# Two of the seven products of the first FFN matmul get a second level of Strassen's scheme, from the second group of tokens on

## The chip, the cores and the metric

The kernel runs on one core of one Trainium2 chip. The metric is the device time of one execution in microseconds (us); lower is better. Before the change the median of three runs is 941.86 us (941.83 to 941.86). Everything is float32.

## The reference

The program is a state-space convolution along the sequence, a routed low-rank FFN, and a residual:

```python
u = conv(x * mask, k) * mask              # x: 64 x 64 x 1024, one kernel per head
xf = u.reshape(4096, 1024)
scores = xf @ Wr.T                        # 64 experts
top_vals, top_idx = top_k(scores, 16)
G = zeros(4096, 64).at[rows, top_idx].set(softmax(top_vals))
h = einsum('nd,krd->nkr', xf, A)          # first FFN matmul: 4096 x 1024 by 1024 x 1024
out = einsum('nkr,kdr->nd', h * G[:, :, None], B) * 2   # second FFN matmul
return x + out
```

## The kernel before, in words

The 4096 tokens are worked in eight groups `g` of 512 (eight heads by 64 batches). For each group the kernel makes the convolution (`conv`), the gates (`gates`, `spread_gates`) and the first FFN matmul (`first`, which runs `seven`). When all groups are through, a second stage (`second`) does the second FFN matmul; the change does not alter its work.

**The first FFN matmul** of a group multiplies the 1024 x 1024 matrix A with the group's 1024 x 512 activations `y`. It uses one level of Strassen's scheme in Winograd's form: A and `y` are cut into 2 x 2 blocks, and seven products of a 512 x 512 left factor with a 512 x 256 right factor take the place of eight. The left factors are the list `wa`; they are made once, partly by DMAs that accumulate, issued from GpSimd (`third_sum`, `fourth_sum`, L230 to L239). The right factors `rf` are four blocks of `y` and their sums `t1`, `t2`, `t4` and `b12`, made on VectorE for each group (`right_factors`).

`seven` is called twice per group, for `j` = 0 and 2: each call does 256 of the 512 rows of every product. In one call a product is eight `nc.tensor.matmul`s (two row blocks of 128 by four blocks of the contraction), each with a 128 x 128 stationary block and 256 moving columns, into one PSUM bank of the four of pool `ps_f`. In the profile each such matmul stands as two MATMUL records and two LDWEIGHTS records, so one product of one `j` is 16 MATMULs (L687). The order in a call is product 1 (bank `c11`), 6, 2 (added to `c11`), 7, 5 (bank `c12`), 4, 3 (added to `c12`). VectorE takes the banks up as they end: `u2 = p1 - p6` (L709), `u3 = p7 + u2` (L716), `c22 = -u3 - c12` (L503), then in `finish` `u3 = p4 - u3` (L492) and `u2 = c12 + u2` (L1052).

`finish` multiplies the four blocks by the gates: one on VectorE (`first_quarter`, L1041), three on GpSimd (L1034). It puts them, and four sums of them (`sums`, VectorE, L492), into the tile `hg`, of which there is one buffer, and stores `hg` to HBM by DMAs from GpSimd's queue (`store`, L1037). The first write to the next `hg` waits until those stores have landed.

**The order of the work.** A scheduling layer fixes each engine's instructions in one static order at build time; each engine runs its own in that order and waits on semaphores. The generators `first` and `conv` are stepped alternately, so that TensorE goes through convolution matmuls of group g+1 between products of group g. Around the change TensorE's order in the middle groups is: the transposes of the gate scores (`psc`, L959), the rest of the products for `j` = 2, the first products of the next group, the convolution's matmuls (`pc`, L828, L836, L851) for head pairs 0 and 1, more products, `pc` for pairs 2 and 3, the state matmuls (`pu`, L742) of the following group, the score matmuls (`psh`, L947), again `pu`, and `psc`.

VectorE's order holds, in the same span: the choice of 16 experts out of `psc` (L961 to L984), the recursion of the states (L786), `right_factors`, the uptake of the products, the tables of the next kernels (`rf`, `rk`, `rsn`, `bt`, and for three of the groups `f`, `k`, `w`), and the uptake of the convolution `y = pc * mask` (L862), which frees the banks that `pu` is written to.

GpSimd's queue holds, in order: the DMAs that make the left factors, then for each group the eight loads of spread gates (`gx`, L1007), the gate multiplications and the stores. In group 0 the order of `first_quarter` is pinned (`late_gates`).

Of the kernel before, what the change touches and what calls it, by code (L numbers as in the profile page):

```python
# [107 lines left out]
def body(ctx: ExitStack, tc, x, xo, lens, par, dvec, dgrp, at, bm, wt, cst, out):  # L108
# [18 lines left out]
    fp = pool(ctx, "fp", 2, "left")  # L127
    gp = pool(left, "gp", 1, "left")
    tq = pool(left, "tq", 1, "left")
    ids = pool(ctx, "ids", 1, "right")  # L130
    const = pool(right, "const", 1, "right")
    xp = pool(right, "xp", 4, "right")
# [369 lines left out]
    def stt(o, a, s, o1, b, o2):  # L502
        V.scalar_tensor_tensor(out=o, in0=a, scalar=s, in1=b, op0=o1, op1=o2)  # L503
        return o
# [169 lines left out]
        tt(t4, b21, t2, ALU.subtract)  # L674
        return b11, b21, b22, t4, t1, t2, b12

    def seven(fac, rf, j, name, finish, second_early=False):

        def product(n, bank=None, more=False):
            first = bank is None
            if first:
                bank = ps_f.tile([P, 2, HT], F32, tag="pf", name=f"{name}_{j}_{n}")
            for ii in range(2):
                for k in range(KH):
                    nc.tensor.matmul(  # L687
                        bank[:, ii, :],
                        lhsT=fac[n - 1][:, k, (j + ii) * P : (j + ii + 1) * P],
                        rhs=rf[n - 1][:, k, :],  # L690
                        start=(first and ii == 0 and k == 0),
                        stop=(ii == 1 and k == KH - 1 and not more),
                        skip_group_check=True,
                    )
            return bank

        def new(t, n=0):
            return fp.tile([P, 2, HT], F32, tag=t, name=f"{name}_{j}_{t}{n}")

        c11 = product(1, more=True)  # L700
        p1 = new("p", 1)
        marks["p1"] = nc.scalar.copy(p1, c11)
        yield
        if second_early:
            product(2, c11)
            yield
        p6 = product(6)
        u2 = new("u2")
        marks["u"] = V.tensor_tensor(out=u2, in0=p1, in1=p6, op=ALU.subtract)  # L709
        yield  # L710
        if not second_early:
            product(2, c11)
            yield
        p7 = product(7)
        u3 = new("u3")
        marks["u"] = V.tensor_tensor(out=u3, in0=p7, in1=u2, op=ALU.add)  # L716
        yield
        c12 = product(5, more=True)
        c22 = new("p", 5)
        stt(c22, u3, -1.0, ALU.mult, c12, ALU.subtract)  # L720
        yield
        p4 = product(4)
        yield
        product(3, c12)
        finish(j, c11, u2, u3, c12, p4, c22)
        yield


    begun = {}
# [284 lines left out]

    hg_dram = dram.tile([NG, P, 7, KH, HT], F32, tag="hg", name="hg_dram")

    def first(g, y, spread):
# [4 lines left out]
        if g:  # L1024
            rf[:] = right_factors(v, f"ty{g}_")

        def finish(j, c11, u2, u3, c12, p4, c22):
            hg = hp.tile([P, 7, 2, HT], F32, tag="hg", name=f"hg_{g}_{j}")

            def gate(m, s):  # L1030
                return spread[m, j][:, :, s * HT : (s + 1) * HT]
# [1 line left out]
            def gt_(o, a, b, op):  # L1033
                G.tensor_tensor(out=o, in0=a, in1=b, op=op)  # L1034

            def store(a, b):
                nc.gpsimd.dma_start(hg_dram[g, :, a:b, j : j + 2, :], hg[:, a:b])  # L1037

            b11, b21, b22, t4, t1, t2, b12 = (hg[:, n] for n in range(7))
            def first_quarter():  # L1040
                i = V.tensor_tensor(out=b11, in0=c11, in1=gate(0, 0), op=ALU.mult)  # L1041
                if late_gates:
# [4 lines left out]
            if not late_gates:  # L1047
                first_quarter()
            gt_(b22, c22, gate(1, 1), ALU.mult)
            tt(u3, p4, u3, ALU.subtract)  # L1050
            gt_(b21, u3, gate(1, 0), ALU.mult)
            marks["u"] = V.tensor_tensor(out=u2, in0=c12, in1=u2, op=ALU.add)  # L1052
            gt_(b12, u2, gate(0, 1), ALU.mult)
            if late_gates:
                first_quarter()
            store(0, 3)

            def sums():
                tt(t1, b11, b12, ALU.subtract)
                tt(b12, b22, b12, ALU.subtract)  # L1060
                tt(t2, b22, t1, ALU.add)
                tt(t4, b21, t2, ALU.subtract)
                store(3, 7)

            unsummed.append(sums)

        for j in range(0, KH, 2):
            for n, _ in enumerate(seven(wa, rf, j, f"h{g}", finish, g + j == 0)):
                if n == 1:
                    sum_factors()  # L1070
                yield
                if n == 1 and len(rf) == 2:

                    rf[:] = right_factors(v, f"ty{g}_")

    unsummed = []

    def sum_factors():
        while unsummed:
            unsummed.pop()()  # L1080


    def second_level(f, e):
# [12 lines left out]

    def load_factor(sg, n, halves):
        for gg in range(2):
            queued(halves[gg], hg_dram[2 * sg + gg, :, n - 1])

    def second_sums(r, u1, u2, u4, pinned=False):

# [249 lines left out]
    for g in range(NG):  # L1352
        ex = gates(g, y)
        if g:
            spread = {}
            for _ in steps:
                pass
            if g + 1 == NG:
                right.close()
                wpb = pool(ctx, "wpb", 1, "right")  # L1360
                wb_quarters = quarters(wpb, bm, "wb", nc.sync)
                ahead(products, 13 - done[0])
                spread_gates(g, ex, spread)
            for _ in products:
                pass
            products, done = counted(first(g, y, spread)), [0]
        if g + 1 == NG:
            break
        ahead(products, (1, 3)[g] if g < 2 else 2)
        spread_gates(g, ex, spread)  # L1370
        if g == 0:
# [140 lines left out]
```

## Time and profile before

| | |
|---|---|
| median of three runs | 941.86 us |
| the profiled execution, its own time | 941.79 us |
| span of its instructions | 940.0 us |
| granted TensorE clock | 1.00 throughout |
| MATMULs of the first FFN matmul (L687) | 1792, 224 for each group |
| first FFN matmul on the chain that ended last | 39% of the span |
| second FFN matmul (L1272) on that chain | 35% |

Times in the profile are in us unless marked ns. PE is TensorE's matmuls, PEld its weight loads, which run beside matmuls; DVE is VectorE, ACT ScalarE, POOL GpSimd, SP the queue of SyncE. A name such as h<-y,was reads: written, then read, with numbers left out; h are the banks of the first FFN matmul, waa and was the left factors, ty and y the right factors, s the states. A group's line gives the count, the busy time, the mean duration in ns of one, and the idle time of the engine before them with what ended it. Durations of back-to-back instructions overlap, so what one costs in a full queue is the step from its start to the next start, not its duration. The chain that ended last is followed back from the last instruction, at each step to what released it.

### The profile page before, as it was taken

How to read it: one execution, taken by the hardware profiler on the slowest of the kernel's cores; microseconds unless marked ns; L12 is line 12 of the kernel's file. 1: busy time of each engine (PE TensorE's matmuls, PEld its weight loads, DVE VectorE, ACT ScalarE, POOL GpSimd, SP SyncE). 2: the span in 40 equal slices, each digit the busy share in tenths (PEclk: the TensorE clock that was granted, in tenths of full speed). 3: DMA queues.
4: the chain of work that ended last, by engine and by line, in shares of the span. 5: the costliest groups of instructions: out<-in, count | busy, mean ns of one | idle time of the engine just before them, and what ended most of it. 6: DMA issues, size and time to landing. Idle time of an engine off the chain costs nothing.

```text
span 940.0 us, 14255 instructions
## 1 busy us (share of the span) xinstructions
PE 929.5 (99%) x5384; PEld 743.2 (79%) x5384; DVE 741.0 (79%) x1725; ACT 164.1 (17%) x314; POOL 337.0 (36%) x284
## 2 busy tenths in 40 slices
PE   7999999999999999999999999999999999999998
PEld 2576768688588588588588788888888888888887
DVE  8899798797996995995892497879856866785674
ACT  5343233411411411510300000000000000000000
POOL 0113213052052052052052032356746555764555
PEclk9999999999999999999999999999999999999999
DMA  8635335347454444444242463754672574358332
GB/s 291 186 87 168 107 110 156 108 126 189 125 144 154 124 138 159 125 128 169 90 131 101 152 246 124 255 203 140 212 275 79 191 270 155 110 205 307 95 123 101
DMA packets 72298, 149.47 MB, mean 159 GB/s; under 512 B 10054, under 2 KB 21030, under 8 KB 72230
## 3 DMA queue, kind: packets, MB, share of 16 engines
q1 hardware_dynamic: 52546, 99.65, 32.1%
q0 software_dynamic: 16864, 47.22, 16.0%
q10 hardware_dynamic: 2820, 1.70, 0.6%
q8 instruction: 42, 0.69, 0.3%
q14 instruction: 26, 0.21, 0.1%
HBM read 100.13 MB, written 47.33 MB: 157 GB/s over the span
## 4 chain that ended last, share of the span: by engine, by line
PE 93%; DVE 6%; issue 0%; DMA 0%; ACT 0%; DVEq 0%
PE h L687 39%; PE s L1272 35%; PE pu L742 5%; PE pc L851 4%; PE psh L947 3%; PE pc L828 3%; PE pc L836 1%; DVE bt L492 1%; DVE hg L492 1%; DVE f L492 1%; DVE f L503 0%; PE psc L959 0%; PE pb L440 0%; PE last L1272 0%; DMA par_sb<-in_par 0%
## 5 line engine op out<-in xcount | busy, mean ns | idle before, releaser
L786 DVE SCALAR_TENSOR_TENSOR s<-s,turn 128x64 f32<-128x64 f32 (+1 forms) x432 | 122.8, 330 | 2.8 <-ACT s L747 2.3
L687 PE MATMUL h<-y,waa 128*128 128x256 f32 x512 | 116.7, 380 | 0.0
L687 PE MATMUL h<-y,was 128*128 128x256 f32 x512 | 116.2, 379 | 0.0
L687 PE MATMUL h<-ty,was 128*128 128x256 f32 x512 | 116.0, 379 | 0.0
L687 PEld LDWEIGHTS h<-y,waa 128*128 128x128 f32 x512 | 96.3, 190 | 15.0 <-issue 1.9
L687 PEld LDWEIGHTS h<-ty,was 128*128 128x128 f32 x512 | 97.1, 190 | 13.9 <-issue 0.8
L687 PEld LDWEIGHTS h<-y,was 128*128 128x128 f32 x512 | 96.8, 190 | 13.7 <-DVE b L503 0.4
L1034 POOL TENSOR_TENSOR hg<-h_p,gx 128x512 f32<-128x512 f32 x16 | 35.6, 2223 | 141.6 <-DVE h_p L503 107.1
L1007 POOL DMA_DIRECT2D gx<-gt_dram x56 | 33.9, 618 | 145.1 <-DMA gt_dram<-gt 145.1
L1286 ACT COPY p<-s 128x512 f32<-128x512 f32 x28 | 16.4, 585 | 312.4 <-PE s L1272 312.4
L1034 POOL TENSOR_TENSOR hg<-h_u,gx 128x512 f32<-128x512 f32 x32 | 45.1, 1409 | 63.8 <-DVE h_u L492 36.6
L1131 POOL TENSOR_TENSOR o<-o,acc_a 128x512 f32<-128x512 f32 x32 | 47.6, 1506 | 41.4 <-ACT acc_a L1149 32.5
L687 PE MATMUL h<-ty,waa 128*128 128x256 f32 x256 | 58.4, 381 | 0.0
L687 PEld LDWEIGHTS h<-ty,waa 128*128 128x128 f32 x256 | 48.2, 190 | 8.3 <-DVE rsn L492 0.8
L742 PE MATMUL pu<-x,bt 128*64 128x448 f32 x256 | 53.0, 546 | 0.4
L862 DVE TENSOR_TENSOR y<-pc,mask 128x512 f32<-128x512 f32 x64 | 40.2, 680 | 16.4 <-PE pc L851 16.4
L1131 POOL TENSOR_TENSOR o<-o,b_room 128x512 f32<-128x512 f32 x32 | 49.1, 1555 | 9.8 <-DVE b_room L492 9.8
L492 DVE TENSOR_TENSOR o<-o,s 128x512 f32<-128x512 f32 x50 | 34.1, 681 | 23.0 <-PE s L1272 17.9
L1037 POOL DMA_DIRECT2D hg_dram<-hg x32 | 25.6, 800 | 67.4 <-DVE hg L492 46.6
L1131 POOL TENSOR_TENSOR o<-o,u 128x512 f32<-128x512 f32 x36 | 45.3, 1282 | 10.0 <-DVE u L492 9.7
L492 DVE TENSOR_TENSOR hg<-hg 128x512 f32<-128x512 f32 x64 | 42.4, 682 | 4.7 <-POOL hg L1034 4.3
L1272 PE MATMUL s<-qy,wbs 128*128 128x256 f32 x192 | 44.1, 379 | 0.0
(275 smaller groups left out, 1678.8 us busy)
## 6 DMA issues: line engine op xcount, KB each, us to landing
x<-in_x SPq DMA_DIRECT2D x32, 512.0 KB
hg_dram<-hg POOLq DMA_DIRECT2D x16, 1024.0 KB, 6.0
o<-in_xo SPq DMA_DIRECT2D x64, 256.0 KB
out<-o SPq DMA_DIRECT2D x63, 256.0 KB
gx<-gt_dram POOLq DMA_DIRECT2D x56, 256.0 KB, 4.8
qy<-hg_dram SPq DMA_DIRECT2D x28, 512.0 KB
r<-hg_dram SPq DMA_DIRECT2D x26, 512.0 KB
hg_dram<-hg POOLq DMA_DIRECT2D x16, 768.0 KB, 4.5
```

What stands on the lines that cost most here:

```text
L492: V.tensor_tensor(out=o, in0=a, in1=b, op=o_)
L687: nc.tensor.matmul(bank[:, ii, :], lhsT=fac[n - 1][:, k, (j + ii) * P : (j + ii + 1) * P], rhs=rf[n - 1][:, k, :], start=(first and ii == ...
L742: nc.tensor.matmul(pu[hh * NS : (hh + 1) * NS, :], lhsT=bt[:, i, (1 - c) * P + hh * NS : (1 - c) * P + (hh + 1) * NS], rhs=xt[:, hh, : NCH ...
L786: return V.scalar_tensor_tensor(out=o, in0=a, scalar=scalar, in1=b, op0=op0, op1=op1)
L828: nc.tensor.matmul(pcs[hh][half_of(e, 1), chunks(e)], lhsT=toep[:, 2 * i + hh, HP:], rhs=xt[:, hh, chunks(e)], start=True, stop=False, ski ...
L851: m = nc.tensor.matmul(pcs[hh][half_of(e, late), into], lhsT=w[o : o + NS, c, i, seg : seg + HP], rhs=s[o : o + NS, c, of].rearrange("p k ...
L862: marks["y"] = V.tensor_tensor(out=y[:, :, i // 2, 2 * (i % 2) + hh, :], in0=pcs[hh].rearrange("p (k b) -> p k b", b=NB), in1=mask, op=ALU ...
L947: nc.tensor.matmul(phalf[o : o + NE, :], lhsT=wt_sb[:, d, :], rhs=yf[:, d, :], start=(d < 2), stop=(d >= NBLK - 2),)
L1007: i = queue.dma_start(gx[:, ii, :], gt_dram[g, c * n : (c + 1) * n, :].unsqueeze(1).to_broadcast([n, RANK, TOK]),)
L1034: G.tensor_tensor(out=o, in0=a, in1=b, op=op)
L1131: tc.keep_in_program_order(G.tensor_tensor(out=o, in0=a, in1=b, op=op_))
L1272: nc.tensor.matmul(bank[:, ii, :], lhsT=left_[i - 1][:, k, ii * P : (ii + 1) * P], rhs=right_[i - 1][:, k, :], start=(first and ii == rows ...
```

## The change

From group 1 on (`LOW_FROM`), products 7 and 4 are no longer done as 512 x 512 by 512 x 256 in two calls. Each is done once per group, as a whole, by a second level of the same scheme (`low`): seven products of a 256 x 256 left factor with a 256 x 128 right factor. Each of the seven is four matmuls, with 128 moving columns in place of 256. The other five products stay as they were.

For this:

- `left_factors` makes the left factors of the second level for `wa[6]` and `wa[3]` once, in group 0, by fourteen DMAs from GpSimd's queue: for each, three copies and an accumulation, two more accumulations, and a last one (in place, after group 0 has used the factor) that is issued at the start of group 1. The first twelve stand on the queue ahead of the `gx` loads of group 0.
- `low_rights` makes the right factors on VectorE: four sums of 128 x 256 for each of the two products in each group.
- `low` does the seven small products and hands their banks to `early` and `late`: seven more VectorE instructions of 128 x 256 for each, and one copy on ScalarE.
- `seven` is one generator over both `j`. Product 7 is done at `j` = 0 and its result kept in two `u3` tiles; product 4 is begun after `j` = 0 and its second half is finished among the products of `j` = 2 (`open_`).
- The gated block `b21` and the sum `t4` come later; they are multiplied and stored apart (`done`, `last_sum`). `hg` has six places in place of seven, each half is stored by four DMAs in place of two, and the order of the factors in HBM follows `SLOT`.
- A pool `lop` holds the new factors, and `dynamic_dma_scratch_size` is 2048 in place of its default.

```diff
+    def left_factors(n):
+        f, h = wa[n - 1], L // 4
+        e = lop.tile([P, 3, 2, h], F32, tag=f"e{n}", name=f"low_{n}")
+        a11, a12, a21, a22 = f[:, :2, :h], f[:, 2:, :h], f[:, :2, h:], f[:, 2:, h:]
+        s1, s2, s4 = e[:, 0], e[:, 1], e[:, 2]
+        for o, a in ((s1, a21), (s2, a11), (s4, a12)):
+            add(o, a)
+        for o, a in ((s1, a22), (s2, s1), (s4, s2), (a21, a11)):
+            add(o, a, accum_op=ALU.add)
+            yield
+    def low_rights(r, name):
+        e = lop.tile([P, 3, 2, H2], F32, tag="r", name=name)
+        tt(u1, r11, r12, ALU.subtract)
+        tt(u2, r22, u1, ALU.add)
+        tt(r12, r22, r12, ALU.subtract)
+        tt(u4, r21, u2, ALU.subtract)
+    def low(n, rights, name, early, late):
+        c11 = product(1, more=True)
+        nc.scalar.copy(v2, c11[:, :, :H2])
+        q6 = product(6)
+        tt(v2, v2, q6[:, :, :H2], ALU.subtract)
+        early(v2)
+        q7 = product(7)
+        tt(v3, q7[:, :, :H2], v2, ALU.add)
+        product(2, c11)
+        late((0, 0), c11[:, :, :H2], None, None)
+        yield
+        c12 = product(5, more=True)
+        late((1, 1), c12[:, :, :H2], v3, v2)
+        q4 = product(4)
+        late((1, 0), q4[:, :, :H2], v3, v3)
+        product(3, c12)
+        late((0, 1), c12[:, :, :H2], None, None)
...
+            steps_ = iter(())
+            if lows and not j:
...
+                steps_ = low(7, low_rights(rf[6], f"{name}_r7"), name, early, late)
+                next(steps_)
+                yield j
...
+            if lows and j:
+                for half, v in zip((lo_, hi_), fourth_of):
+                    tt(u3[:, :, half], v, u3[:, :, half], ALU.subtract)
...
-            store(0, 3)
+            store(0, 2, 0)
...
+            def last_sum():
+                tt(b11, b21, t2, ALU.subtract)
+                store(0, 1, 6)
+            def done(u3):
+                gt_(b21, u3, gate(1, 0), ALU.mult)
+                store(2, 3, 2)
+                unsummed.extend((sums, last_sum))
...
+        if g == 0:
+            made_left = [left_factors(n) for n in (7, 4)]
+            for steps_ in made_left:
+                ahead(steps_, 3)
```

## The prediction

> **What bounds the kernel now.** I read the page first, its busy shares and its chain, and then asked for the waits of TensorE. From the page and from the whole chain in order of time:
>
> ```profile
> PE 929.5 (99%) x5384; PEld 743.2 (79%) x5384; DVE 741.0 (79%) x1725; ACT 164.1 (17%) x314; POOL 337.0 (36%) x284
> DVE  8899798797996995995892497879856866785674
> PE 93%; DVE 6%; issue 0%; DMA 0%; ACT 0%; DVEq 0%
> ...
> 68.60 0.88 PE pb L440 x8
> 253.41 34.53 PE h L687 x160
> ```
>
> TensorE is busy 99% of the span, so a matmul left out shortens the run if nobody else becomes late. The digits of DVE say that somebody could: up to the 24th slice VectorE is near 80 to 90%. A table by stretch makes that plain (span, then busy time of PE, PEld, DVE, ACT, POOL, clock, DMA):
>
> ```profile
> 223.00:294.00 71.00, 70.88 (x470) 54.36 (x470) 61.13 (x168) 18.46 (x33) 18.64 (x18) 1.00 0.46 141
> 436.00:507.00 71.00, 71.00 (x476) 54.52 (x469) 54.91 (x149) 9.09 (x18) 18.99 (x19) 1.00 0.37 120
> ```
>
> One group takes 71 us of TensorE and 55 to 61 us of VectorE. That is not yet slack to spend: both run in a fixed order, and VectorE's free time may lie elsewhere than where TensorE waits for it. The chain across one turn of a middle group shows that VectorE is already on the path there:
>
> ```profile
> 229.93 0.04 DVE h_u L1052
> 230.54 2.35 DVE bt L492 x2
> 242.24 0.61 DVE y L862
> 242.89 3.23 PE pu L742 x16
> 252.72 0.59 PE psc L959 x4
> 253.41 6.69 PE h L687 x31
> ```
>
> From the last product at 229.93 to the end of the first uptake of `y` VectorE works 12.9 us without a break; `pu` needs that bank and starts at 242.89, just as TensorE's own matmuls run out. The same chain stands at 301 and at 372.
>
> **The gain on TensorE.** A whole product is 2 x 16 MATMULs per group; at 34.53 / 160 = 0.2158 us that is 6.91 us. By the second level it is 7 x 4 matmuls, 56 records of 128 columns. No row has such a matmul with an ordinary stationary block. Nearest are the transposes of L440, which also move 128 columns and load a new 128 x 128 block each time:
>
> ```profile
> L687 PE MATMUL h<-y,waa x512: 379/379/483, 39.6 to 583.0; 128*128 128x256 f32 x171
> L440 PE MATMUL pb<-cst_sb,b x32: 270/272/332, 19.8 to 174.7; 128*128 128x128 f32 x32
> L687 PEld LDWEIGHTS h<-y,waa x512: 186/190/192, 39.6 to 582.8; 128*128 128x128 f32 x171
> L440 PEld LDWEIGHTS pb<-cst_sb,b x32: 137/139/143, 19.8 to 174.6; 128*128 128x128 f32 x32
> ```
>
> Eight of them take 0.88 us, 0.110 each. Their weight load takes 139 ns, that of a product 190, so this is the lower bound: 56 x 0.110 = 6.16, a gain of 0.75 us a product. Upper bound, if loads followed each other at their full duration: 56 x 0.190 = 10.64, a loss of 3.73. A load seems to cost less than its duration: the first matmul of a product behind other work takes 483 ns, not 379, so a load that nothing covers costs 104 ns, and that fits under 110. I take 0.110: 14 products (two in each of seven groups) x 0.75 = **10.4 us gained**; range +52 to -10.4.
>
> Here a rule speaks against the change. The Trainium skill, page "TensorE: Matmul & The Clock Gate", section "Back-to-back issue gap", says that in pairs of weight load and matmul both set the spacing, and gives some 81 ns at 128 columns where a lone matmul would take 56. By that ratio 0.110 would be 0.16, a product 8.9 us, and the change would lose 28 us on TensorE alone; the transposes, in pairs too, do not show it.
>
> **What VectorE gets.** From its timeline after `psc`, and the group beside it:
>
> ```profile
> 254.26 0.68 DVE L961 TENSOR_REDUCE sc<-psc 128x256 f32<-128x512 f32 x1
> ...
> 257.95 0.41 DVE L492 TENSOR_TENSOR sb<-sb,sc 128x256 f32<-128x256 f32 x1
> 258.28 0.41 DVE L492 TENSOR_TENSOR sa<-sc,m 128x256 f32<-128x256 f32 x1
> 258.62 0.67 DVE L1041 TENSOR_TENSOR hg<-h,gx 128x512 f32<-128x512 f32 x1
> ...
> 265.67 0.67 DVE L503 SCALAR_TENSOR_TENSOR h_p<-h_u,h 128x512 f32<-128x512 f32 x1
> ```
>
> From start to start a 128 x 256 instruction costs 0.335 us and a 128 x 512 one 0.60 (258.62 to 259.22). Per group the two small schemes bring 22 of the first kind, `j` = 2 brings two more and one `u3 + u2` of 0.60, and four of 0.60 go (L716 and `p4 - u3`, twice): 24 x 0.335 + 0.60 - 2.40 = 6.2 us. 61.1 + 6.2 = 67.3 of a turn of 69.5: by sums it fits, with 3% to spare. So I went along both engines' new order and looked at each place where TensorE waits for VectorE.
>
> *a. The second half of product 4, behind `psc`.* TensorE now comes from `psc` and its small transpose (0.55 us), through small products 5 and 4 (0.88 each) and half of product 6 (1.73), to small product 3 at 4.04 us after `psc`'s start; it needs `late((1, 1))` on VectorE, which the order puts behind the choice of experts. VectorE starts that 1.54 us after `psc` (252.72 to 254.26), needs 3.5 us to 257.75, and 0.335 for the uptake: 5.4. TensorE waits 1.4 us; in the fourth such turn, where `sc` starts 1.08 after `psc`, 0.9. Before, 3 x 3.46 us of products covered the same work.
>
> *b. `c22` before product 3 of `j` = 2.* Before, product 4 (3.46 us) lay between product 5, which feeds `c22`, and product 3, which overwrites its bank. Now 1.30 us of product 1 of the next group do. VectorE reached `c22` 11.4 us after `sc` (254.26 to 265.67). In the new order 1.0 of small uptakes, 0.60 of `last_sum` and 0.60 and more of `u3` and `u2` come ahead: 14.1, and 0.6 to do it, 16.3 after `psc`. TensorE is there at 14.8 + 1.4 = 16.2. But `last_sum` stands in VectorE's queue too, and waits for GpSimd's multiplication of `b21` (1409 ns, L1034), which can start only when the last uptake is done; only 0.86 us of recursion lies between. About 0.8 more, and all behind it on VectorE waits with it: 0.9 us.
>
> *c. `u2` before small product 7.* From `c22` to `u2` VectorE has 11.0 us in the new order (four sums of `right_factors` at 1.14, `sums`, `low_rights` of 1.3), TensorE 10.8, with small product banks to be freed by it: 0.7, with one 1.86 us instruction for 1.14 where GpSimd is multiplying.
>
> *d. The uptake of `y`.* The 12.9 us chain above gets four small uptakes and loses L709: 12.9 + 1.34 - 0.60 = 13.6. On TensorE three small products (2.64) replace product 6 (3.46): 12.1 in place of 12.96. It waits 1.5 us, in the three turns that have the `f` tables.
>
> Sum: three turns at 1.4 + 0.9 + 0.7 + 1.5 = 4.5 are 13.5; one turn without tables 0.9 + 0.9 + 0.7 = 2.5; the first two groups and the last have the same pairs in other places: 2.2 each for the two, 1.6 for the last, by half of the others. Together **24 us lost**; bounds 9 (only *d* and half of *a*) and 38 (each added instruction with two SBUF inputs once beside a multiplication, as bt<-rsn,rf at 231.13 took 1.68 for 0.60, twice a group).
>
> **GpSimd's queue in group 0.** Twelve DMAs come ahead of the `gx` loads:
>
> ```profile
> 49.63 0.88 POOL L239 DMA_DIRECT2D was<-was  x1 [1.03 <-DMA was<-in_at]
> 67.62 4.83 POOL L1007 DMA_DIRECT2D gx<-gt_dram  x8 [17.11 <-DMA gt_dram<-gt]
> ```
>
> Each factor is a chain of copy, accumulation, accumulation, each waiting for the landing before it. At 4.8 us to landing (`gx`, page, 256 KB) two chains take 29 us: from 50.5 to 80 at least, where `gx` now starts at 67.6. At 3.5, the shortest landing of `gx` in that stretch, 72. VectorE stands at `first_quarter` of group 0 (73.69, pinned) until `gx` lands, so 4 to 14 us longer, with the recursion for group 1 behind it. TensorE needs that recursion at 92.72 and has it at 86.98: 5.7 are covered. It costs 0 to 8 us; I take 4, the middle. The two accumulations in place of group 1 cost nothing: 1.5 us of issue in a queue idle for 64% of the span, under two products; uncovered, 10 us once. Two more stores for each half of `hg`, 0.8 us of issue each, lie in the same idle time, except the wait in *b*. ScalarE's two copies (0.35 us, 83% idle) are covered by the small product between. The later `t4` is read in the second stage only.
>
> The smaller DMA scratch (2048) shows in no row. If it lets GpSimd issue a transfer only after the one before has landed, a store holds GpSimd for its 6.0 us landing (page) and not for 0.8 of issue; two stores stand ahead of multiplications that VectorE waits for, so up to 10 us a group, 70 in all. Lower end 0: eight `gx` loads, the densest run of transfers, need 8 x 0.7 us of issue and 4.8 of landing, and few are open at once. I take 0, by these denser rows, and count the upper end among the cases left out above.
>
> **Sum.** The profiled execution took 941.79 us, 0.07 under the median, span 940.0: 941.8 - 10.4 + 24 + 4 - 2 (a wait of TensorE gives VectorE time to catch up, so the places do not add in full; half a place in four turns) = **957 us**, 1.6% slower.
>
> **Rivals.** *VectorE keeps up* (the other side). Its place is *a* to *d*: if TensorE's waits stay under 10.4 us in all, that is under 1.5 us a group, the change wins. For it speaks that 67.3 fits in 69.5; against, that *a* and *d* are chains counted from TensorE's own instructions, where a mean share helps nothing. With *d* alone (4.5): 936. *Weight loads set the pace*: at 0.150 a record TensorE loses 14 x 1.49 = 21, its slower products then cover part of *a* to *c* (12 left): 974; at 0.190, 1000. For it the 190 ns, against it 104 ns. *The factors' DMAs decide*: at 14 us of delay, 8 lost at the states and the rest handed on to `y` of group 1, with the steady waits as above: 966. *It cancels*: waits near 10 us, no change.
>
> **Chances.** Forecast 0.55; VectorE keeps up 0.15; weight loads 0.10 (half of it above 974); DMAs 0.15; cancels 0.05. From 943 to 974 lie the forecast, the DMAs and half of the weight loads, about 0.8; the bounds 9 and 38 us of the steady waits give 942 and 971. Faster by over 0.2%, which is about what a measurement here can tell from no change, 0.15; within it 0.05; slower 0.8.
>
> **What would show it.** Right: waits of PE for DVE that were not there, in the stretch 223 to 507 some 4 us a group, at small product 3 of product 4, at product 3 of `j` = 2, at `pu`; records of 128 columns spaced 0.11; DVE above 90% there; `gx` of group 0 issued past 72. Wrong: a stretch of PE without gaps and groups of 69.5 us (VectorE keeps up), or 128-column records spaced 0.15 and more with VectorE no busier.

## The result, and the profile after

The changed kernel takes **1012.84 us** (median of four runs, 1011.2 to 1016.1) against 941.85 us before: a ratio of 1.076, interval 1.073 to 1.079. It is 71 us slower. The forecast was 957 us, slower, with a range up to 974; the direction was right and the size was not.

The page of the changed kernel, its busy times, VectorE's slices and the granted clock, and the shares of the chain that ended last:

```profile
PE 944.7 (94%) x5720; PEld 759.4 (75%) x5720; DVE 778.2 (77%) x1872; ACT 169.6 (17%) x328; POOL 372.8 (37%) x330
DVE  8984889698796796797688459879975785686674
PEclk9999899998999998999999999999999999999999
PE 56%; DVE 24%; POOL 5%; issue 2%; DMA 2%; ACT 1%; DVEq 0%; POOLq 0%
```

TensorE was 99% busy and is now 94%. VectorE is busy for 37 us more but for no larger a share. Of the chain, VectorE has 24% where it had 6%, and GpSimd, which was not on it, 5%. And in the row of the clock some slices are no longer full: the mean granted clock is 0.98, before it was 1.00. So TensorE waits, and after some waits it also runs more slowly.

One turn of a middle group, from `psc` to the next `psc`; first of the kernel before, then of the changed one (span; busy time of PE, PEld, DVE, ACT, POOL; granted clock, DMA share, GB/s):

```profile
252.65:323.80 71.15, 71.02 (x472) 54.52 (x470) 61.03 (x167) 18.46 (x33) 18.59 (x18) 1.00 0.46 139
```

```profile
282.00:361.74 79.74, 72.47 (x520) 56.64 (x518) 65.31 (x188) 19.32 (x35) 21.84 (x22) 0.98 0.41 124
```

The turn is 8.6 us longer. VectorE works 65.3 of 79.7 us: it isn't the bound by its sum. What TensorE waited for in the changed kernel, over the whole span (total, times, longest). In the kernel before it has no wait of this list in the middle groups:

```profile
PE h L721 <- DVE h_r L493: 16.3, 6, 3.1
PE h L760 <- DVE h_p L504: 8.0, 7, 2.9
PE pc L992 <- DVE s L927: 7.9, 2, 7.5
...
PE h L721 <- DVE ty L504: 4.6, 4, 1.3
PE h L721 <- DVE h_u L793: 4.6, 6, 1.0
...
PE pu L883 <- DVE y L1003: 3.1, 3, 1.0
```

Three of these were forecast: `ty` L504 is step *a* (1.28 us a turn, forecast 1.4), `h_p` L504 is `c22`, step *b* (0.94 in a middle turn, forecast 0.9), `y` L1003 is step *d* (1.03 in three turns, forecast 1.5). The largest is `h_r`, the right factors of product 7 at the second level, 2.8 to 3.1 us in each of five turns, with some 0.9 for `u2` (L793) just behind; this is the place of step *c*, forecast at 0.7. VectorE's own waits and GpSimd's queue in that turn say where it comes from:

```profile
DVE hg L493 <- POOL hg L1177: 4.4, 1, 4.4
```

```profile
298.00 1.82 POOL L1148 DMA_DIRECT2D gx<-gt_dram  x3 [5.35 <-DMA gt_dram<-gt]
299.82 4.92 POOL L1177 TENSOR_TENSOR hg<-h_p,gx 128x512 f32<-128x512 f32 x1
304.68 0.61 POOL L1148 DMA_DIRECT2D gx<-gt_dram  x1
305.29 0.76 POOL L1180 DMA_DIRECT2D hg_dram<-hg  x1
306.06 1.28 POOL L1177 TENSOR_TENSOR hg<-h_u,gx 128x512 f32<-128x512 f32 x1
...
308.90 1.28 POOL L1177 TENSOR_TENSOR hg<-h_u,gx 128x512 f32<-128x512 f32 x1
```

Read it from the end. VectorE's sums of `hg` start at 310.21, when the multiplication of `b12` (the row at 308.90) is done. GpSimd had `c22` from 299.5 on and needs 10.7 us from there to the end of `b12`: loads of `gx`, stores, and the multiplication of `b22`, which takes 4.92 us where the others take 1.28, while VectorE runs the four sums of right factors beside it. The right factors of product 7 stand on VectorE's queue behind the sums.

In the kernel before, these sums hardly waited. VectorE's sums of `hg` over the whole span, before and after (the last number is what they waited for GpSimd):

```profile
L492 DVE TENSOR_TENSOR hg<-hg 128x512 f32<-128x512 f32 x64 | 42.4, 682 | 4.7 <-POOL hg L1034 4.3
L493 DVE TENSOR_TENSOR hg<-hg 128x512 f32<-128x512 f32 x64 | 42.6, 682 | 33.0 <-POOL hg L1177 27.7
```

Yet GpSimd's queue was much the same. The turn of the kernel before, GpSimd and then VectorE; and VectorE in the changed one:

```profile
267.16 3.92 POOL L1034 TENSOR_TENSOR hg<-h_p,gx 128x512 f32<-128x512 f32 x1
271.02 1.81 POOL L1007 DMA_DIRECT2D gx<-gt_dram  x3
272.85 1.28 POOL L1034 TENSOR_TENSOR hg<-h_u,gx 128x512 f32<-128x512 f32 x1
274.43 0.81 POOL L1037 DMA_DIRECT2D hg_dram<-hg  x1 [0.30 <-POOL hg L1034]
275.83 1.26 POOL L1034 TENSOR_TENSOR hg<-h_u,gx 128x512 f32<-128x512 f32 x1 [0.60 <-DVE h_u L1052]
...
275.06 0.68 DVE L1052 TENSOR_TENSOR h_u<-h,h_u 128x512 f32<-128x512 f32 x1
277.43 0.68 DVE L492 TENSOR_TENSOR hg<-hg 128x512 f32<-128x512 f32 x1
```

```profile
298.85 0.68 DVE L504 SCALAR_TENSOR_TENSOR h_p<-h_u,h 128x512 f32<-128x512 f32 x1
...
304.13 1.70 DVE L493 TENSOR_TENSOR ty<-y,ty 128x1024 f32<-128x1024 f32 x1
310.21 0.69 DVE L493 TENSOR_TENSOR hg<-hg 128x512 f32<-128x512 f32 x1 [4.39 <-POOL hg L1177]
```

Before, GpSimd was free for `b12` 8.9 us after `c22` (done at 266.34, free at 275.24) and even waited 0.6 us for VectorE's `u2`; now it gets to `b12` after 9.4 us. What moved is VectorE. Before, it came to the sums 11.8 us after the start of `c22` (265.67 to 277.43), with some 5 us of recursion in between (272.08 to 275.06, and from 275.66 on); the new order has none there, and VectorE is done with the right factors 7.0 us after `c22`. It comes 4.8 us earlier to a result that comes no earlier, and waits 4.4.

Then the clock. Four stretches of 3.41 us around that wait, in the changed kernel (the column after POOL is the granted clock):

```profile
308.04:311.45 3.41, 1.76 (x13) 1.47 (x11) 1.24 (x3) 0.13 (x1) 3.39 (x6) 1.00 0.60 218
311.45:314.86 3.41, 1.13 (x8) 0.97 (x8) 3.41 (x9) 1.53 (x2) 1.68 (x3) 1.00 0.88 266
314.86:318.27 3.41, 3.31 (x15) 3.31 (x16) 3.02 (x13) 0.00 (x0) 0.18 (x1) 0.50 0.71 278
318.27:321.69 3.42, 3.42 (x19) 3.03 (x18) 0.61 (x2) 0.00 (x0) 0.00 (x0) 1.00 0.00 0
```

The third stretch runs at half clock: TensorE is busy and does half the work (sixteen records of 128 columns that start at 314.96 follow each other at 0.216 us; at full clock it is 0.111), so a wait of 3.1 us costs about 4.8. In the whole span there are 41 us at half clock, and half of that, 20 us, is lost.

Group 0 lost as much. GpSimd's queue there, with the factor DMAs (L690, the rows between left out) ahead of the `gx` loads, and what waits for them:

```profile
50.05 2.54 POOL L690 DMA_DIRECT2D low<-was  x3
56.41 1.22 POOL L690 DMA_DIRECT2D low<-was  x1 [3.82 <-DMA low<-was]
...
80.28 0.85 POOL L690 DMA_DIRECT2D low<-low  x1 [3.79 <-DMA low<-low]
80.87 3.90 POOL L1148 DMA_DIRECT2D gx<-gt_dram  x6
```

```profile
DVE hg L1184 <- DMA gx<-gt_dram: 15.2, 1, 15.2
```

`gx` starts at 80.87, before it was 67.62: 13.3 us later. VectorE stands for 15.2 us, TensorE for 7.5 (`pc` <- `s`), then for 2.9 and 2.2, and 17 us of that stretch run at half clock. The second `psc` comes at 146.7 in place of 126.9, before a single product by the second level was done.

The added MATMULs themselves are as fast as taken. Eight of them follow each other at the spacing of the transposes:

```profile
362.34 1.06 PE L721 MATMUL h<-h_r,low 128*128 128x128 f32 x8
363.23 1.06 PE L721 MATMUL h<-h_r,waa 128*128 128x128 f32 x8
```

From start to start 0.89 for eight, 0.111 each: a product takes 6.23 us for 6.91 before.

### The profile page after: what moved, and what is told of

It reads as the page before. It is cut to its first block, busy times and chain, and to the rows that moved or that the text cites. A ratio compares the mean times of both kernels' runs of the same rounds, so it can differ in the third digit from the quotient of the medians.

```text
span 1009.4 us, 15219 instructions
## 1 busy us (share of the span) xinstructions
PE 944.7 (94%) x5720; PEld 759.4 (75%) x5720; DVE 778.2 (77%) x1872; ACT 169.6 (17%) x328; POOL 372.8 (37%) x330
## 4 chain that ended last, share of the span: by engine, by line
PE 56%; DVE 24%; POOL 5%; issue 2%; DMA 2%; ACT 1%; DVEq 0%; POOLq 0%
PE s L1424 33%; PE h L760 10%; PE h L721 6%; DVE s L927 5%; POOL hg L1177 3%; DVE hg L493 2%; PE pc L992 2%; PE pc L969 2%; PE pu L883 1%; DVE s_more L927 1%; DVE h_u L493 1%; POOL gx L1148 1%; DMA gt_dram<-gt 1%; PE psh L1088 1%; DVE y L1003 1%
## 5 line engine op out<-in xcount | busy, mean ns | idle before, releaser
L760 PE MATMUL h<-y,waa 128*128 128x256 f32 x512 | 119.9, 385 | 0.0
L927 DVE SCALAR_TENSOR_TENSOR s<-s,turn 128x64 f32<-128x64 f32 (+1 forms) x432 | 116.5, 314 | 2.0 <-ACT s L888 1.3
L1177 POOL TENSOR_TENSOR hg<-h_p,gx 128x512 f32<-128x512 f32 x16 | 38.9, 2432 | 174.3 <-DVE h_p L504 170.5
L760 PE MATMUL h<-y,was 128*128 128x256 f32 x288 | 68.4, 391 | 8.0 <-DVE h_p L504 8.0
L1180 POOL DMA_DIRECT2D hg_dram<-hg x64 | 43.6, 681 | 87.3 <-DVE hg L493 31.3
L760 PEld LDWEIGHTS h<-y,was 128*128 128x128 f32 x288 | 54.4, 194 | 19.4 <-DVE h_p L504 11.1
L1003 DVE TENSOR_TENSOR y<-pc,mask 128x512 f32<-128x512 f32 x64 | 40.6, 682 | 16.5 <-PE pc L992 16.5
L992 PE MATMUL pc<-s,w 64*64 64x192 f32 (+1 forms) x768 | 42.4, 368 | 7.9 <-DVE s L927 7.9
L721 PE MATMUL h<-h_r,low 128*128 128x128 f32 x224 | 30.4, 279 | 16.3 <-DVE h_r L493 16.3
L883 PEld LDWEIGHTS pu<-x,bt 128*64 128x64 f32 x256 | 17.4, 137 | 35.7 <-issue 16.7
```

The costliest lines, as they stand in the source:

```text
L721: nc.tensor.matmul(bank[:, ii, :H2], lhsT=LOW[n][i - 1][:, k, ii * P : (ii + 1) * P], rhs=rights[i - 1][:, k, :], start=(first and ii == 0 ...
L760: nc.tensor.matmul(bank[:, ii, :], lhsT=fac[n - 1][:, k, (j + ii) * P : (j + ii + 1) * P], rhs=rf[n - 1][:, k, :], start=(first and ii == ...
L883: nc.tensor.matmul(pu[hh * NS : (hh + 1) * NS, :], lhsT=bt[:, i, (1 - c) * P + hh * NS : (1 - c) * P + (hh + 1) * NS], rhs=xt[:, hh, : NCH ...
L927: return V.scalar_tensor_tensor(out=o, in0=a, scalar=scalar, in1=b, op0=op0, op1=op1)
L992: m = nc.tensor.matmul(pcs[hh][half_of(e, late), into], lhsT=w[o : o + NS, c, i, seg : seg + HP], rhs=s[o : o + NS, c, of].rearrange("p k ...
L1003: marks["y"] = V.tensor_tensor(out=y[:, :, i // 2, 2 * (i % 2) + hh, :], in0=pcs[hh].rearrange("p (k b) -> p k b", b=NB), in1=mask, op=ALU ...
```

## The experiments

All against the kernel before on the same chip. "Shorter" means: by the medians. First, what each part costs by itself.

**The frame alone.** No second level and no factor DMAs.

```diff
-    LOW_FROM = 1
+    LOW_FROM = NG
-            if g == 1:
-                for steps_ in made_left:
-                    ahead(steps_, 2)
...
-            made_left = [left_factors(n) for n in (7, 4)]
-            for steps_ in made_left:
-                ahead(steps_, 3)
```

> No product by the second level and no factor DMAs; what stays of the change: the one generator over both j, hg with six places, the later b21 and t4, four stores for each half in place of two, the smaller DMA scratch. If these cost nothing, as the prediction put it: 942, within 1 us. If the smaller scratch or the added stores hold GpSimd's queue (the upper end in the prediction, 10 us a group): up to 1012, with GpSimd's transfers spaced by their landing.

Measured: 946.2 us, ratio 1.005 (1.003 to 1.006). So the frame isn't free: 4.3 us. Waits that the kernel before did not have: `pb` for `y` 1.7 us in group 1, `pu` for `y` 1.2 us in group 2, `ey` 0.9 us in the second stage.

**`t4` in a place of its own**, on top of that:

```diff
-            hg = hp.tile([P, 6, 2, HT], F32, tag="hg", name=f"hg_{g}_{j}")
+            hg = hp.tile([P, 7, 2, HT], F32, tag="hg", name=f"hg_{g}_{j}")
...
-                tt(b11, b21, t2, ALU.subtract)
-                store(0, 1, 6)
+                tt(t4, b21, t2, ALU.subtract)
+                store(6, 7, 6)
```

> frame_only, with t4 in a seventh place of hg instead of the place of b11. Theory A (the 4 us of frame_only come from t4, which VectorE may write only when the store of b11 has landed, with the uptake of y of group 1 behind it): 942 to 943. Rival (the smaller DMA scratch or the added stores cost it): 946 as before.

Measured: 946.4 us (ratio 1.003 to 1.006): no gain. The wait in group 1 did go, the second `psc` came at 126.95, as before the change. But in group 2 it came back larger. VectorE's wait in that turn, and TensorE's:

```profile
DVE hg L1184 <- DMA hg_dram<-hg: 6.6, 1, 6.6
```

```profile
PE pu L883 <- DVE y L1003: 2.9, 1, 2.9
```

There is one `hg`, and the next one's first write waits for its last store. That store is now the one of `t4`, and GpSimd issues it at 212.3, after the `gx` loads; before, the last store of the half was issued at 208.0. A stretch of 3.41 us at half clock follows that wait. So the theory held in group 1, where the place of `t4` cost 1.7 us, and missed that its late store costs as much and more in group 2.

**The smaller DMA scratch**, in the kernel before:

```diff
-    nc = bacc.Bacc("TRN2", target_bir_lowering=False, num_devices=1)
+    nc = bacc.Bacc("TRN2", target_bir_lowering=False, num_devices=1, dynamic_dma_scratch_size=2048)
```

> The kernel before with the smaller DMA scratch (2048) and nothing else. Theory A (as the prediction put it, 2048 costs nothing where no more than eight small loads are open at once): 941.8 to 942.2. Rival (it is part of the 4 us of frame_only): 943 or more.

> The kernel before with a DMA scratch of 1024. Theory A (the scratch limits how much can be open at once on GpSimd's queue; the eight gx loads are the densest run, so gaps of 1 to 2 us appear between their issues, which in the kernel before follow each other at 0.6 us): slower by some us, 944 to 960, with issue gaps on GpSimd's queue and none at 2048. Rival (the gaps in late6 come from its factor copies, in rows of 1 KB, alone): 942.

Measured: 941.88 with 2048 (ratio 1.000, 0.999 to 1.001), 942.25 with 1024 (1.001, 1.000 to 1.002; not told from no change). The mechanism is real all the same. Of the kernel with 1024, GpSimd's waits that nobody released, and the `gx` loads of group 0:

```profile
POOL gx L1007 <- issue: 28.7, 21, 4.1
...
67.65 1.89 POOL L1007 DMA_DIRECT2D gx<-gt_dram  x3 [12.63 <-DMA gt_dram<-gt]
71.59 0.59 POOL L1007 DMA_DIRECT2D gx<-gt_dram  x1 [2.05 <-issue]
```

With 2048 there are two such gaps, 1.3 us in all, with the default none. In this kernel GpSimd has the time. So 2048 is cleared for the kernel before, as the prediction took it, and the expectation that 1024 would cost 2 us or more was wrong.

**The factor DMAs alone**: the frame with the first twelve of them.

> As frame_only, with the first twelve factor DMAs issued in group 0 and their results never read. Theory A (their two chains of dependent transfers hold the gx loads and with them VectorE and TensorE of group 0): the first transposes of scores after group 0's (psc of group 1) come 18 to 20 us later than before, as in the changed kernel; 942 + 19 = 961. Theory B (the prediction's 4 us; the rest of the 20 belongs to the small products): 946.

Measured: 964.7 us, 18.5 over the frame: theory A. TensorE waits 7.1 us for the states, 4.3 for `c22`, and 10.2 us run at half clock. By the second `psc` 15.6 of the 18.5 are lost (144.43 for 128.82 in the frame alone).

**The two chains side by side**, in the changed kernel:

```diff
         for o, a in ((s1, a21), (s2, a11), (s4, a12)):
             add(o, a)
+        yield
...
-            for steps_ in made_left:
-                ahead(steps_, 3)
+            for _ in range(4):
+                for steps_ in made_left:
+                    ahead(steps_, 1)
```

> The changed kernel, with the twelve factor DMAs in the same place of the queue but the two factors' chains side by side: six copies, then the accumulations in turn. Theory A: each landing is waited for once for both factors, so gx starts near 66 in place of 80.9, the 19.8 us of group 0 vanish: 1012.8 - 19 = 994, clock of TensorE 1.00 up to 140. Rival (the transfers themselves, not the waiting in the queue, take the time): gx still at 76 or later, 1005 or more.

Measured: 1002.8 us, 10 shorter, between the two. `gx` starts at 68.1 and the wait of 7.5 us is gone. In its place a new one, of VectorE and behind it of TensorE:

```profile
DVE hg L493 <- DMA hg_dram<-hg: 6.8, 1, 6.8
```

```profile
PE pb L441 <- DVE y L1004: 8.1, 1, 8.1
```

VectorE writes `t4` into the place of `b11` and waits for its store; the two accumulations in place stand on the queue ahead of that store and its data lands some 10 us after GpSimd began to issue it, where the stores of `hg` take about 5 (the page's medians are 4.7 and 5.2). The prediction had these accumulations at nothing, "uncovered, 10 us once".

**Now the steady turns. The sums of `hg` behind `u2`:**

```diff
-            if n in (1, 3 if j and g >= LOW_FROM else 2):
+            if g > 1 and not j:
+                if n == 2:
+                    with tc.issue_after(marks["u"].ins):
+                        sum_factors()
+            elif n in (1, 3 if j and g >= LOW_FROM else 2):
                 sum_factors(1)
```

> The changed kernel, with the sums of hg from the second half of a group (groups 2 on) put on VectorE's queue behind u2 of the next group instead of ahead of the right factors of product 7. Theory A (VectorE stands 4.4 us before these sums for GpSimd's multiplication of b12, which its queue reaches late behind the multiplication of b22, gx loads and a store; TensorE waits 3.1 + 0.9 us for the right factors behind it and then runs 3.4 us at half clock): the wait of TensorE for h_r goes, and the half clock with it; 4 to 5.5 us in each of five turns and 1 in the last: 985 to 991. Rival (VectorE is short of time anyway, so TensorE waits as long at the next uptake): 1005 or more.

Measured: 1002.4 us, 10 shorter, where 22 or more was expected. VectorE's wait for GpSimd is gone, but TensorE now waits 2.5 to 2.9 us for `u2`. VectorE's right factors of product 7 in that kernel:

```profile
306.00 1.90 DVE L493 TENSOR_TENSOR h_r<-y 128x256 f32<-128x256 f32 x1
308.09 0.41 DVE L493 TENSOR_TENSOR h_r<-y,h_r 128x256 f32<-128x256 f32 x1
308.42 0.41 DVE L493 TENSOR_TENSOR y<-y 128x256 f32<-128x256 f32 x1
308.76 1.98 DVE L493 TENSOR_TENSOR h_r<-y,h_r 128x256 f32<-128x256 f32 x1
```

Two of four take 1.9 us in place of 0.41. GpSimd multiplies `b21` and `b12` just then (306.33 and 309.17, 1.28 each). So GpSimd costs VectorE twice: by being late, and by holding it up while it works.

**Product 2 ahead of the small products of 7**, to cover the wait with TensorE's own work:

```diff
             if lows and not j:
+                product(j, 2, c11)
+                yield j
                 u3 = new(j, "u3")
...
-            if not early_:
+            if not early_ and not (lows and not j):
                 product(j, 2, c11)
```

> The changed kernel, with product 2 (3.46 us, needs nothing new from VectorE) ahead of the first half of product 7's small products instead of between its halves. Theory A (what is late is the single step: the right factors of product 7 and u2 come 4.0 us too late for TensorE, and a wait that long also halves its clock for 3.4 us): the waits there shrink from 3.1 + 0.9 to about 1.2, the half clock goes, and about 1 us of wait appears at small product 3, where product 2 gave cover: 3.5 us less in each of five turns, 995. Rival (VectorE is short of time over the whole turn, so what is covered here is waited for at the next uptake): 1008 or more.

Measured: 1007.1 us, 6 shorter, near the rival. The wait moved by one step: 0.8 for `u2` and 2.3 to 2.6 at the next small product, behind VectorE's sums. Cover on TensorE did not help here: VectorE is held up by a third engine, and the wait comes back one step later.

**The gates of the second half on VectorE.**

```diff
-                G.tensor_tensor(out=o, in0=a, in1=b, op=op)
+                (V if j and 0 < g < NG - 1 else G).tensor_tensor(out=o, in0=a, in1=b, op=op)
```

> The changed kernel, with the three gate multiplications of the second half of groups 1 to 6 moved from GpSimd to VectorE, 1.8 us more work there in each group. Theory A (VectorE loses more by GpSimd than it saves: 4.4 us of waiting for b12, and in the kernel with the sums pinned two of its additions took 1.9 us in place of 0.42 while GpSimd was multiplying): VectorE gets to u2 about 3 us earlier, the wait of 3.1 us falls under 1.5 and the half clock goes: 4 to 5 us less in each of five turns, 988 to 994. Rival (VectorE is simply short of time): 1.8 us more in each of six turns, 1020 to 1024.

Measured: **981.0 us, 31.8 shorter**, more than expected, although VectorE has three more instructions a group. The same turn:

```profile
274.35:348.36 74.01, 70.65 (x520) 54.84 (x518) 66.47 (x191) 19.34 (x35) 14.45 (x19) 1.00 0.45 134
```

VectorE is busier than in the changed kernel (66.5 for 65.3 us) and the turn is 5.7 us shorter, all at full clock. TensorE's waits in it are those of *a*, *b* and *d* and no other:

```profile
PE h L721 <- DVE ty L504: 1.3, 1, 1.3
PE pu L883 <- DVE y L1003: 1.0, 1, 1.0
PE h L760 <- DVE h_p L504: 0.9, 1, 0.9
```

**The gate of `b12` alone on VectorE**, to part the late queue from the collisions:

```diff
-            gt_(b12, u2, gate(0, 1), ALU.mult)
+            if j and 0 < g < NG - 1:
+                tt(b12, u2, gate(0, 1), ALU.mult)
+            else:
+                gt_(b12, u2, gate(0, 1), ALU.mult)
```

> The changed kernel with the multiplication of b12 alone, in the second halves of groups 1 to 6, on VectorE; b22 and b21 stay on GpSimd. Theory A (the 32 us that gates_vec gave back were the wait of VectorE for b12 at the end of GpSimd's queue): nearly all of it comes back with this one alone, 981 to 986. Theory B (they were the collisions of GpSimd's multiplications with VectorE's additions): b22 and b21 still collide, at most a third comes back, 1000 or more.

Measured: 993.0 us, 19.8 of the 31.8. Neither theory alone: this one multiplication gives back about two thirds. It is not a clean parting, as it also takes one of the three multiplications from beside VectorE. In the turns of this kernel `b22` and `b21` still collide: VectorE's own multiplication of `b12` takes 2.17 us beside GpSimd's of `b21`, and TensorE waits 1.6 us a turn for `u2`.

**Do the costs add?** The chains side by side and the gates on VectorE together, first with the accumulations in place behind the `gx` loads of group 1:

```diff
-            if g == 1:
-                for steps_ in made_left:
-                    ahead(steps_, 2)
...
-        ahead(products, (1, 3)[g] if g < 2 else 2)
+        ahead(products, 1 if not g else 2)
         spread_gates(g, ex, spread)
+        if g == 1:
+            for steps_ in made_left:
+                ahead(steps_, 2)
```

> The changed kernel with three edits: the factors' chains side by side, the accumulations in place behind the gx loads of group 1, and the gate multiplications of the second halves of groups 1 to 6 on VectorE. Theory A (the 70 us are three separate costs: 4 for the frame, 18.5 for the factor DMAs in group 0 with the halved clock, 32 for GpSimd's multiplications with the halved clock, and 16 for the waits a, b and d less the saving): only frame and waits stay: 981 - 18.5 = 962 to 964, clock 1.00 nearly throughout. Rival (the costs cover one another, as side by side alone brought 10 and not 19): 970 or more.

Measured: 981.6 us, no better than the gates alone. But TensorE's order in group 1 had changed with that edit, and it waited 8.8 us for the landing of the accumulations. With TensorE's order as it was, and the accumulations behind the store of the sums:

```diff
-        ahead(products, (1, 3)[g] if g < 2 else 2)
+        ahead(products, 1 if not g else 2)
+        if g == 1:
+            for steps_ in made_left:
+                ahead(steps_, 2)
+            ahead(products, 1)
```

> The three edits of combo, with the accumulations in place now behind the store of the sums of group 0's second half: TensorE's order is that of side by side alone (in combo it had changed, and TensorE waited 8.8 us for the landing of these accumulations). Theory A (the costs are separate once no new wait takes the place of the old): 962 to 966. Rival (group 0 and 1 are bound by the transfers, wherever they are put): 971 or more.

Measured: **964.5 us** (ratio 1.022 to 1.027), as theory A had it. So 16.5 of the 18.5 us of group 0 can be had back, and they add to the 31.8.

**The second level where VectorE has room**, in the last two groups:

```diff
-    LOW_FROM = 1
+    LOW_FROM = 6
...
         spread_gates(g, ex, spread)
+        if 0 < g < 5 or g == LOW_FROM:
+            for steps_ in made_left:
+                ahead(steps_, 2 if g == LOW_FROM else 1)
```

> The second level in the last two groups alone, where VectorE has no tables and no recursion of a next group to make; the factor DMAs spread over groups 1 to 6 behind the gx loads, one step for each group, so that no landing is waited for; product 2 first; t4 in its own place; DMA scratch 1024. Theory A (the saving of 1.3 us a group is there where VectorE has room): 942.0 - 2.6 + 1 to 2 of waits = 940.5 to 941.5, just faster than before. Rival (the chain of uptakes is too long for TensorE in these groups too): 944 to 948.

> The second level in the last two groups alone, the factor DMAs spread over groups 1 to 6 behind the gx loads, DMA scratch 2048 and t4 in the place of b11 as in the change, the gate multiplications of the second halves of groups 5 and 6 on VectorE. Theory A (in late6 it was the scratch of 1024 that held GpSimd's transfers, up to 5 us between two issues, and the waits of groups 2 to 5 came from that): these go; 946 for the frame - 2.6 + 2 to 4 of waits: 944 to 948. Rival (the spread factor DMAs themselves hold the queue): 960 or more.

Measured: 982.4 and 957.4 us. The first has a scratch of 1024: gaps of up to 5.1 us between the factor DMAs, and a wait of 7.9 us of TensorE for `c22` in a group without any second level. The second changes the scratch, the place of `t4`, the place of product 2 and the gates at once, so how much of the 25 us between them is the scratch stays open. It has 8 us of such gaps in all, and is still 11 us over the frame (12.1 in the two profiled executions): 4.3 in group 2, where the store of `t4` stands behind two factor DMAs until 219.3, VectorE waits 7.6 us for it and `pu` 3.4 us for `y`; 1.6 in the turn before the last, 6.2 after it (`h_r` 1.7, `ey` 2.6, `acc_a` 1.7), where the saving is 2.6 at most. No version here beats the kernel before.

## Why the prediction was wrong

Three steps failed: *c*, which had no wait for GpSimd in it (0.7 us a turn forecast, some 4 measured, and half clock behind it); the DMAs of group 0 (4 us forecast, 18.5 measured); and the price of a wait, which left out that TensorE's clock halves behind it. The runs part the 71 us, each term a difference of two medians. The terms add up by construction; that the second and the third are separate costs is shown by the 964.5 us of the run that takes both out, where they would give 962.5.

| | us | forecast |
|---|---|---|
| frame (frame alone less before) | 4.3 | 0 |
| factor DMAs in group 0 (with them less without) | 18.5 | 4 |
| GpSimd beside VectorE in the steady turns (changed kernel less gates on VectorE) | 31.8 | *c*, in the next row |
| waits *a*, *b*, *d* and others, less the saving of TensorE (gates on VectorE less factor DMAs alone) | 16.3 | 24 - 10.4 - 2 = 11.6 |

- **Step *c* failed at GpSimd.** The prediction gave VectorE 11.0 us from `c22` to `u2`, all of it VectorE's own work, with one sum stretched beside a multiplication ("1.86 us", which stands in no row; the stretched sum of that turn, at 270.47, took 1.69). It took 16.0 (298.85 to 314.83), since the sums of `hg` stand in this stretch and wait 4.4 us for `b12`. The prediction should have walked GpSimd's queue as it walked the other two: behind `c22` come the multiplication of `b22`, stretched to 4.92 us, then a load, a store, `b21`, a store, a load and `b12`. The rows of the kernel before had nearly the same 9 us up to `b12` (above); there, recursion on VectorE covered them. The collisions had been priced (the upper bound of 38 us), but as a far end and not as the likely case.
- **Step *b*** came out at 0.94 for 0.9, in part by luck. Most of its forecast was a wait of VectorE for GpSimd's `b21` ("About 0.8 more"). That wait did not occur: the multiplication ended at 290.53, and VectorE was busy with the recursion until its sum started at 291.00. VectorE reached `c22` late by its own work, 16.9 us after `psc`.
- **Steps *a* and *d*** were right in place, 1.28 for 1.4 and 1.03 for 1.5.
- **The saving.** 0.111 us for a record of 128 columns, as taken: right at the level of the product (0.68 for 0.75). By the ratio that the Trainium skill, page "TensorE: Matmul & The Clock Gate", section "Back-to-back issue gap", gives for pairs of weight load and matmul, it would have been 0.16, an estimate; the trace of these MATMULs decides for 0.111. In a turn less of it is left: TensorE's busy time falls from 71.02 only to 70.65 with the gates on VectorE. Every wait adds some 0.16 us of pipeline to it (a MATMUL of 128 columns ends 0.27 us after its start and the next could start at 0.11), and the first matmuls behind a wait are some 0.1 us slower (the eight records from 287.56 take 0.99 us, not 0.89).
- **A steady turn by itself** came out right because two misses cancel. Without GpSimd's part it is 2.9 us longer than before (74.01 for 71.15), where the forecast, with the 0.7 of *c* in it, has 4.5 of waits less 1.5 of saving, 3.0; but the waits were 3.2 and the saving 0.4.
- **The DMAs of group 0** failed at the choice in the middle. The prediction had "4 to 14 us longer" and "5.7 are covered"; `gx` was issued 13.3 us later, and 13.3 - 5.7 = 7.6 is the wait measured (7.5). What followed it was not priced: the waits of 2.9 and 2.2 us behind, and the clock. The rival "the factors' DMAs decide" had the mechanism; its 966 is near the 964.7 of that part alone only by chance, as it holds the steady waits too.
- **The clock** was missing altogether. Each wait was priced at its length. The Trainium skill, same page, section "HAM oscillation — how this bites in real kernels", warns that a TensorE that idles for longer than some 3.4 us is throttled again. Here a wait of 1.75 us was enough in one run (below). Of the 31.8 us in the steady turns some 12 are half clock (24 us of such stretches), of those in groups 0 and 1 some 8.
- **The frame** was costed at nothing, "in the same idle time". The idle time is there; but the last store of a half is what the next `hg` waits for, and that store became later.
- **The sum** has a slip: its terms, 13.5 + 2.5 + 2 x 2.2 + 1.6, make 22.0 and not 24, so by them the forecast is 955. It does not bear on the miss.
- *VectorE keeps up* would have needed waits under 1.5 us a group. Even with GpSimd out of the way they are 3.2.

With GpSimd's gates moved and the DMAs put side by side the kernel takes 964.5 us. That is near the case that the 957 describes, plus the 4.3 of the frame.

## What to carry to other kernels

A wait for a third engine is priced by walking that engine's queue from the moment its input is ready, with all that stands in it, and not by the duration of the instruction waited for. A change that lets one engine come earlier makes waits at another whose work is as long as before. Where two engines hold each other up, it can pay to let one of them do the work, even the busier one: three more instructions a group on VectorE shortened this run by 32 us. And on a TensorE that is 99% busy, a wait of 2 us or more can be followed by 3.4 us at half clock, so here several short waits were cheaper than one long one.

## What the hardware showed

**The clock follows a grid.** The half-clock stretches in a profile all start on multiples of 3.413 us from the first of them, and last one, two or three such pieces (3.41, 6.83 or 10.24 us). Cutting the spans of the twelve kernels that have such stretches into these pieces, from 20 us on, and looking at TensorE's busy share in a piece that ran at full clock:

| busy share of a piece of 3.41 us | next piece at half clock |
|---|---|
| under 0.40 | 43 of 43 |
| 0.40 to 0.49 | 8 of 18 |
| 0.49 to 0.80 | 0 of 140 |

So it isn't the length of a wait that decides but how much of it falls into one piece. In the kernel with the sums pinned, a wait of 1.84 us was followed by half clock, and one of 2.5 us, which comes in four turns, in two of them. The shortest wait that was followed by it with no other wait beside it took 1.75 us, in the kernel that takes 964.5 us. That the runs of the changed kernel spread over 5 us where those before agree within 0.1 would fit a grid that lies differently in each run; it was not tested.

**VectorE and GpSimd hold each other up for whole instructions** where VectorE adds two operands from SBUF: 1.90 and 1.98 us in place of 0.41, ending 0.3 us after GpSimd's multiplication, and the other way round GpSimd's multiplication of `b22` at 4.0 to 5.1 us in the turns of the changed kernel while VectorE's sums follow each other, and at 1.3 without them. The Trainium skill, page "SBUF — State Buffer", section "Who interferes with whom", says that a VectorE instruction with two inputs from SBUF contends with a GpSimd instruction that reads SBUF, that the shared pair of ports is an exclusive lock, and that the order of issue decides who is blocked. The durations agree. The order can't be read from these rows: the sum that took 1.90 is recorded from 306.00, ahead of the multiplication at 306.33, and yet it was the one held.

**A scratch that is too small for GpSimd's transfers shows as gaps with no releaser**: none with the default, 1.3 us in all with 2048, 28.7 us at the `gx` loads alone with 1024. In the kernel before, where GpSimd has time, neither shows in the run's time; in the changed kernel's group 0 two gaps of 0.8 and 1.7 us stand between the last `gx` loads. No run has the changed kernel with the default, so what they cost there is not shown.
